# Turning the softmax rows of the first and the last attention tiles on TensorE, and storing the last block tile by tile

## The chip, the cores and the metric

The kernel runs on one core of a Trainium2 chip. The metric is the device time of one execution in microseconds. Engines are named as in the profile: PE is TensorE (PEld its weight loads), DVE is VectorE, ACT is ScalarE, POOL is GpSimd, SP is SyncE; a "q" behind a name is that engine's instruction queue, which also issues DMAs.

## The reference

The input x has 2 batches of 2048 rows and 256 columns in float32. Two layers follow one another, each on the layer norm of x:

```
x = x + attn0(xn) + moe(xn)        # layer 0: causal attention, 8 routed + 2 shared SwiGLU experts
x = x + attn1(xn) + chosen(xn)     # layer 1: causal attention, a block on the 255 best rows of each batch

def attn(x):
    q, k, v = x @ Wq, x @ Wk, x @ Wv          # layer 0 with biases, layer 1 with an output product
    s = where(causal, q @ k.T, -inf) / 16
    return softmax(s) @ v
```

## The kernel before

**Attention.** Both layers call one function, `attention` (L236). A tile is 128 query rows of one batch, 16 tiles a batch. `in_turn` (L366) takes batch 0 upwards, tiles 0 to 15, then batch 1 downwards, tiles 15 to 0, so the first and the last tiles are the shortest. The row of tile i has (i + 1) x 128 columns, cut into chunks of up to 512. `scores` (L246) multiplies queries by the normed rows on TensorE (L256), adds the causal mask to the last 128 columns, and lets VectorE scale the chunk into an SBUF buffer `row` (L267; two such buffers); ScalarE takes the exponential over the whole row (L275).

To average the values, the probabilities are needed the other way round, keys on the partitions. This is done without TensorE: `turn` (L299) has GpSimd split the float32 words of each chunk into two planes of 16-bit halves (L306), SyncE transposes both by one DMA (L308), and `join` (L280) puts the halves together as `pT`, one by VectorE (L286) and one by ScalarE (L287). `average` (L314) multiplies `pT` by the values (L321), and VectorE adds the scaled result to x (L333). Averages are held back: the oldest pending tile is averaged once at least three chunks are pending besides the newest tile's (`pending`), so the turning has other tiles' work to lie beside. After the last tile the three tiles still pending are averaged one after the other.

**Work beside it.** `piece` (L292) is called after each chunk and runs steps of generators in `side`: in layer 0, layer norm, values and gate logits of later blocks of 512 rows (`prepare0`, L483), then the routing of the experts; in layer 1, the chosen block of batch 1 and `write_back`. In layer 0 each of the first tiles also lets ScalarE issue two stores that clear scratch memory (`clear_some`, L464, and L438, 768 KB each). `project_q0` (L629) and `project_q1` (L1497) make the queries of a block once its first tile comes.

**What is shared.** PSUM has banks by tag, two for each tag (`bank`, L67): "mm" for projections, transposes and all side work, "sc" and "tr" for scores, "pv" for averages. `evacuate` (L150) copies a bank to SBUF, by VectorE and by ScalarE in turn, counted over the whole program.

**Order.** The program is traced in the order of the code, and a planner then sets the order in each engine's queue from the dependencies and its own estimates. A few dependencies are written by hand: `lead` names the main work, the joins and some DMAs are kept behind it.

**The end.** After `attention` of layer 1 a loop stores the eight blocks of x, 512 KB each, on SyncE's queue (L1521, L1522). Block 4 holds tiles 3 to 0 of batch 1 and is finished last.

Of the kernel before, what the change touches and what calls it, by code (L numbers as in the profile page):

```python
# [9 lines left out]
F32 = mybir.dt.float32  # L10
# [7 lines left out]
P = 128  # L18
B, S, D = 2, 2048, 256
NB = 8  # L20
BPB = NB // B
# [29 lines left out]
def transformer_kernel(ctx: ExitStack, tc: tile.TileContext, a: dict, out: bass.AP):  # L51
    nc = tc.nc
# [14 lines left out]
    def bank(tag):  # L67
        return psum.tile([P, 512], F32, tag=tag, name=f"ps_{tag}")

    x_blocks = []  # L70
# [8 lines left out]
    for g in range(NB):  # L79
        load_x(g, nc.sync)  # L80

    ident = const.tile([P, P], F32, tag="ident", name="ident")
# [5 lines left out]
        out=tri, in_=tri, compare_op=ALU.is_ge, fill=NEG, base=0, pattern=[[-1, P]], channel_multiplier=1  # L88
# [33 lines left out]
    def step():  # L122
        while side:
            traced = nc.cur_bb.bb.instructions
            n = len(traced)
            got = next(side[0], step)
            for i in nc.cur_bb.bb.instructions[n:]:
                behind(i)
            held[0] = got == HOLD
            if got is not step:  # L130
                return
            side.pop(0)
# [17 lines left out]
    def evacuate(dst, src):  # L150

        copies[0] += 1
        if copies[0] % 2:
            nc.vector.tensor_copy(dst, src)
        else:
            nc.scalar.copy(dst, src)
# [76 lines left out]
                nc.tensor.transpose(ps[:, j * P : (j + 1) * P], xn[:, j, c * P : (c + 1) * P], ident)  # L233
            evacuate(xnT[g][:, c, :], ps)

    def attention(pool, tiles, project_q, values, each, shifts=None, filling=()):  # L236

        def scores(b, i):  # L246
            g0 = b * BPB
            qT = queries[g0 + i // 4]
            row = pool.tile([P, S], F32, tag="row", name="row")
            mx = small.tile([P, 4], F32, tag="mx", name="mx")  # L250
            n = (i + 1) * P
            chunks = [(c, min(512, n - c)) for c in range(0, n, 512)]
            for k, (c, w) in enumerate(chunks):
                ps = bank(("sc", "tr")[k % 2])
                for dc in range(2):
                    product = nc.tensor.matmul(  # L256
                        ps[:, :w],
                        lhsT=qT[:, dc, (i % 4) * P : (i % 4 + 1) * P],
                        rhs=xnT[g0 + k][:, dc, :w],
                        start=(dc == 0),  # L260
                        stop=(dc == 1),
                    )
                lead(product)
                if c + w == n:
                    nc.vector.tensor_add(ps[:, w - P : w], ps[:, w - P : w], tri)
                by = 1.0 / 16.0 if shifts is None else shifts[g0 + i // 4][:, i % 4 : i % 4 + 1]
                lead(nc.vector.tensor_scalar(  # L267
                    row[:, c : c + w], ps[:, :w], by, None,
                    op0=ALU.mult if shifts is None else ALU.add, op1=ALU.max, accum_out=mx[:, k : k + 1],
                ))  # L270
                piece()
            nmx = small.tile([P, 1], F32, tag="nmx", name="nmx")
            nc.vector.tensor_reduce(nmx, mx[:, : len(chunks)], AX.X, ALU.max, negate=True)
            total = small.tile([P, 1], F32, tag="total", name="total")
            lead(nc.scalar.activation(row[:, :n], row[:, :n], AF.Exp, bias=nmx, accum_out=total))  # L275
            inv = small.tile([P, 1], F32, tag="inv", name="inv")
            nc.vector.reciprocal(inv, total)
            return b, i, row, inv, chunks

        def join(k, w, across, turned):  # L280

            pT = pool.tile([P, 512], F32, tag="pT", name="pT", bufs=6)
            words = pT[:, :w].bitcast(U16).rearrange("p (n k) -> p n k", k=2)
            flat = across.rearrange("p b n -> p (b n)")
            for i in (
                nc.vector.tensor_copy(words[:, :, 1], flat[:, :w]),  # L286
                nc.scalar.copy(words[:, :, 0], flat[:, w : 2 * w]),  # L287
            ):
                tc.add_manual_dep(i.ins, main[i.ins.engine].name, order, reason="not before it is there")
            turned[k] = pT  # L290

        def piece():  # L292

            pieces[0] += 1
            while joins and joins[0][0] <= pieces[0]:
                join(*joins.pop(0)[1:])
            beside()

        def turn(b, i, row, inv, chunks):  # L299

            turned = [None] * len(chunks)
            for k, (c, w) in enumerate(chunks):
                halves = row[:, c : c + w].bitcast(U16).rearrange("p (n k) -> p n k", k=2)
                planes = pool.tile([P, 1024], U16, tag="planes", name="planes", bufs=4)
                for h in range(2):
                    nc.gpsimd.tensor_copy(planes[:, h * w : (h + 1) * w], halves[:, :, 1 - h])  # L306
                across = pool.tile([P, 8, P], U16, tag="across", name="across", bufs=4)
                lead(nc.sync.dma_start_transpose(across[:, : 2 * w // P, :], planes[:, : 2 * w]))  # L308
                joins.append((pieces[0] + LAG + k, k, w, across, turned))
                if len(joins) == 4:  # L310
                    join(*joins.pop(0)[1:])
            return b, i, turned, inv, chunks

        def average(b, i, turned, inv, chunks):  # L314
            g0 = b * BPB
            pv = bank("pv")
            for k, (c, w) in enumerate(chunks):
                while turned[k] is None:
                    join(*joins.pop(0)[1:])
                for j in range(0, w, P):  # L320
                    product = nc.tensor.matmul(  # L321
                        pv[:, :D],
                        lhsT=turned[k][:, j : j + P],
                        rhs=values[g0 + k][:, j // P, :D],
                        start=(c + j == 0),
                        stop=(c + j == i * P),
                    )
                    if c + j == 0 and filled_up:
                        tc.add_manual_dep(product.ins, filled_up.ins.name, order, reason="the filling first")
                lead(product)  # L330
                piece()
            xt = x_blocks[g0 + i // 4][:, i % 4, :]
            nc.vector.scalar_tensor_tensor(xt, pv[:, :D], inv, xt, op0=ALU.mult, op1=ALU.add)  # L333

        queries = {}
        pending, joins, pieces = [], [], [0]
        filled_up = None
        def meet(tile):

            each(*tile)  # L340
            g = tile[0] * BPB + tile[1] // 4
            if g not in queries:
                queries[g] = project_q(g)

        meet(tiles[0])
        for tile, later in zip(tiles, tiles[1:] + [None]):
            pending.append(turn(*scores(*tile)))
            if later:
                meet(later)
            while sum(len(p[2]) for p in pending[:-1]) >= 3:  # L350
                average(*pending.pop(0))
        filling = iter(filling)
        for late in [*pending, None]:
            last, n = main[mybir.EngineType.PE], len(nc.cur_bb.bb.instructions)
            filled_up = next(filling, None)
            if filled_up:
                for i in nc.cur_bb.bb.instructions[n:]:
                    if i.engine == mybir.EngineType.PE:
                        tc.add_manual_dep(i, last.name, order, reason="not ahead of its turn")
                lead(filled_up)  # L360
            if late:
                average(*late)
        assert next(filling, None) is None
# [14 lines left out]
    with ExitStack() as l0:  # L378
# [336 lines left out]
        def fill_with_first():  # L715

            while side:
                step()
            w1, w2, _, _, xT = fetched[0]
            for h in range(0, 4, 2):  # L720
                for we_in, tag in ((w1, "sc"), (w2, "tr")):
                    first_up[h, tag], product = up(we_in, h, xT, TT, tag)
                    yield product
# [23 lines left out]
            for _ in work_of:  # L747
                pass
        side.append(side0())
        attention(work, in_turn, project_q0, values, before_tile, shifts, fill_with_first())  # L750
        assert next(clearing, None) is None
        while side:
            step()
# [761 lines left out]
        if (b, i) == in_turn[S // P + 1]:  # L1515
            finished.add(0)

    attention(att, in_turn, project_q1, values1, before_tile1)
    while side:
        step()  # L1520
    for g in range(NB):  # L1521
        nc.sync.dma_start(  # L1522
            out[g * 512 : (g + 1) * 512, :].rearrange("(j p) d -> p j d", p=P), x_blocks[g]
        )


_PI = 3.1415925
# [58 lines left out]
```

## Time and profile before

| | |
|---|---|
| time, median of 3 runs | 1511.12 us (1510.91 to 1512.03) |
| the profiled execution's own time | 1507.24 us |
| its span, first to last instruction | 1505.5 us |
| PE busy | 1448.6 us, 96% |
| DVE, ACT, POOL busy | 695.7, 440.0, 407.6 us |
| planes, L306 | 320 copies, 567 ns each |
| joins on ACT, L287 | 160 copies, 677 ns each |
| averages, L321 | 1088 matmuls of 256 columns, 380 ns each, pipelined |
| mean granted TensorE clock | 0.997 of full speed |

The page gives each engine's busy tenths in 40 equal slices of the span. A row of groups has line, engine, operation, output and inputs by the program's names, their shapes and count, then busy time and mean, and the idle time of the engine before them with what ended it. A float32 matmul appears as two instructions. In a timeline a row has its start, its duration, the queue, the line and the operation; "x4" marks several like instructions merged into one row.

### The profile page before, as it was taken

How to read it: one execution, taken by the hardware profiler on the slowest of the kernel's cores; microseconds unless marked ns; L12 is line 12 of the kernel's file. 1: busy time of each engine (PE TensorE's matmuls, PEld its weight loads, DVE VectorE, ACT ScalarE, POOL GpSimd, SP SyncE). 2: the span in 40 equal slices, each digit the busy share in tenths (PEclk: the TensorE clock that was granted, in tenths of full speed). 3: DMA queues.
4: the chain of work that ended last, by engine and by line, in shares of the span. 5: the costliest groups of instructions: out<-in, count | busy, mean ns of one | idle time of the engine just before them, and what ended most of it. 6: DMA issues, size and time to landing. Idle time of an engine off the chain costs nothing.

```text
span 1505.5 us, 17837 instructions
## 1 busy us (share of the span) xinstructions
PE 1448.6 (96%) x5796; PEld 1029.9 (68%) x5796; DVE 695.7 (46%) x2068; ACT 440.0 (29%) x831; POOL 407.6 (27%) x597
## 2 busy tenths in 40 slices
PE   6999999999999999999999999999999998999998
PEld 4566666658888888887665656566675765666665
DVE  6347432343222222222424447766546459666344
ACT  2443333332111111111121121115524433344233
POOL 3554776622111111111201221132013122421132
PEclk9999999999999999999999999999999999999999
DMA  5844665685878989873101011220004435621154
GB/s 157 257 115 112 174 149 129 136 162 149 234 221 221 274 234 301 226 208 102 33 21 43 28 43 35 65 97 29 0 14 115 109 70 123 146 51 24 35 119 101
DMA packets 288528, 182.99 MB, mean 122 GB/s; under 512 B 190928, under 2 KB 263376, under 8 KB 288432
## 3 DMA queue, kind: packets, MB, share of 16 engines
q1 hardware_dynamic: 252608, 133.90, 36.4%
q10 hardware_dynamic: 28192, 27.06, 5.7%
q0 software_dynamic: 7632, 20.86, 4.5%
q8 instruction: 48, 0.79, 0.2%
q14 instruction: 48, 0.39, 0.1%
HBM read 93.14 MB, written 45.14 MB: 92 GB/s over the span
## 4 chain that ended last, share of the span: by engine, by line
PE 29%; issue 10%; DVE 7%; POOL 3%; DMA 2%; ACT 2%; POOLq 0%; ACTq 0%; DVEq 0%; SPq 0%
PE ps_tr L1453 6%; PE ps_sc L1453 6%; PE ps_pv L1472 5%; POOL planes L306 3%; DMA across<-planes 2%; PE ps_mm L1324 2%; PE ps_mm L1286 1%; DVE x L1483 1%; PE ps_sc L256 1%; PE ps_mm L916 1%; PE ps_mm L1307 1%; PE ps_pv L321 1%; PE ps_mm L1390 1%; DVE row L267 1%; PE ps_tr L256 1%
## 5 line engine op out<-in xcount | busy, mean ns | idle before, releaser
L306 POOL COPY planes<-row 128x512 uint16<-128x512 uint16 (+3 forms) x320 | 167.1, 567 | 294.3 <-ACT row L275 280.7
L287 ACT COPY pT<-across 128x512 uint16<-128x512 uint16 (+3 forms) x160 | 106.1, 677 | 218.0 <-DMA across<-planes 209.0
L256 PE MATMUL ps_sc<-xnT,qT 128*128 128x512 f32 (+3 forms) x384 | 161.1, 541 | 2.3 <-ACT qT L638 2.2
L1442 POOL DMA_INDIRECT ya<-sorted_y,place x64 | 62.2, 972 | 307.6 <-DVE x L1483 224.7
L821 DVE SCALAR_TENSOR_TENSOR hid<-ps_tr,be,act 128x256 f32<-128x256 f32 (+1 forms) x144 | 60.9, 465 | 180.1 <-PE ps_tr L706 178.8
L820 ACT ACTIVATE act<-ps_sc,be 128x256 f32<-128x256 f32 (+1 forms) x144 | 58.6, 459 | 280.8 <-PE ps_sc L706 280.8
L321 PE MATMUL ps_pv<-v,pT 128*128 128x256 f32 x544 | 128.1, 381 | 5.5 <-ACT pT L287 4.5
L706 PE MATMUL ps_sc<-xT,rw 128*128 128x256 f32 (+1 forms) x576 | 129.6, 368 | 0.6 <-issue 0.6
L706 PE MATMUL ps_tr<-xT,rw 128*128 128x256 f32 (+1 forms) x576 | 129.4, 367 | 0.0
L321 PE MATMUL ps_pv<-vg,pT 128*128 128x256 f32 x544 | 124.5, 380 | 3.6 <-ACT pT L287 3.2
L698 POOL COPY xT<-xs 128x512 uint16<-128x512 uint16 (+1 forms) x72 | 49.1, 727 | 290.7 <-DMA xs<-sorted_x 265.4
L828 PE MATMUL ps_pv<-rw,hid 128*128 128x256 f32 x544 | 124.9, 382 | 0.0
L1453 PE MATMUL ps_sc<-xnT,sw 128*128 128x512 f32 x256 | 121.9, 594 | 1.8 <-PEq L856 1.8
L1453 PE MATMUL ps_tr<-xnT,sw 128*128 128x512 f32 x256 | 122.0, 593 | 0.0
L321 PEld LDWEIGHTS ps_pv<-vg,pT 128*128 128x128 f32 x544 | 101.8, 189 | 26.6 <-ACT pT L287 6.9
L321 PEld LDWEIGHTS ps_pv<-v,pT 128*128 128x128 f32 x544 | 101.3, 189 | 27.3 <-ACT pT L287 8.0
L1472 PE MATMUL ps_pv<-sw,hid 128*128 128x256 f32 x512 | 117.5, 380 | 0.0
L706 PEld LDWEIGHTS ps_sc<-xT,rw 128*128 128x128 f32 x576 | 105.3, 190 | 14.3 <-POOL xT L698 0.9
L706 PEld LDWEIGHTS ps_tr<-xT,rw 128*128 128x128 f32 x576 | 105.1, 190 | 13.2
L828 PEld LDWEIGHTS ps_pv<-rw,hid 128*128 128x128 f32 x544 | 99.2, 190 | 19.3 <-DVE hid L821 5.7
L1472 PEld LDWEIGHTS ps_pv<-sw,hid 128*128 128x128 f32 x512 | 96.6, 190 | 18.8 <-issue 6.2
L256 PEld LDWEIGHTS ps_sc<-xnT,qT 128*128 128x128 f32 x384 | 69.9, 190 | 56.2 <-issue 43.1
(332 smaller groups left out, 1932.2 us busy)
## 6 DMA issues: line engine op xcount, KB each, us to landing
rw<-in_rw SPq DMA_DIRECT2D x108, 512.0 KB, 4.5
sorted_x<-zero ACTq DMA_DIRECT2D x13, 768.0 KB, 6.3
sorted_y<-y SPq DMA_DIRECT2D x32, 256.0 KB, 4.2
be<-biases SPq DMA_DIRECT2D x36, 132.0 KB, 4.1
table<-xn SPq DMA_DIRECT2D x8, 514.0 KB, 3.4
x<-in_x SPq DMA_DIRECT2D x8, 512.0 KB, 6.9
gains<-zero ACTq DMA_DIRECT2D x8, 512.0 KB, 3.6
gain<-gains SPq DMA_DIRECT2D x16, 256.0 KB, 2.6
```

The costliest lines, as they stand in the source:

```text
L256: product = nc.tensor.matmul(ps[:, :w], lhsT=qT[:, dc, (i % 4) * P : (i % 4 + 1) * P], rhs=xnT[g0 + k][:, dc, :w], start=(dc == 0), stop=( ...
L287: nc.scalar.copy(words[:, :, 0], flat[:, w : 2 * w]),
L306: nc.gpsimd.tensor_copy(planes[:, h * w : (h + 1) * w], halves[:, :, 1 - h])
L321: product = nc.tensor.matmul(pv[:, :D], lhsT=turned[k][:, j : j + P], rhs=values[g0 + k][:, j // P, :D], start=(c + j == 0), stop=(c + j = ...
L698: nc.gpsimd.tensor_copy(words[:, :, :, 1 - k], xs[:, 2 * k : 2 * k + 2, :])
L706: product = nc.tensor.matmul(ps[:, k * n : (k + 1) * n], lhsT=we_in[:, dc, (h + k) * P : (h + k + 1) * P], rhs=xT[:, dc, :], start=(dc == ...
L820: activated = nc.scalar.activation(act, p1[:, at], AF.Silu, bias=b1[:, hc])
L821: nc.vector.scalar_tensor_tensor(hid[:, h + k, :], p2[:, at], b2[:, hc], act, op0=ALU.add, op1=ALU.mult)
L828: product = nc.tensor.matmul(po[:, r, :], lhsT=hid[:, hc, r * P : (r + 1) * P], rhs=w3[:, hc, :], start=(hc == 0), stop=(hc == 3),)
L1442: nc.gpsimd.indirect_dma_start(out=ya, out_offset=None, in_=sorted_y, in_offset=bass.IndirectOffsetOnAxis(ap=place[rank][:, t : t + 1], ax ...
L1453: product = nc.tensor.matmul(ps, lhsT=ww[:, dc, hc * P : (hc + 1) * P], rhs=xnT[g][:, dc, :], start=(dc == 0), stop=(dc == 1),)
L1472: product = nc.tensor.matmul(po[:, :D], lhsT=hid[:, hc, j * P : (j + 1) * P], rhs=w["sw3", n][:, hc, :], start=(hc == 0), stop=(hc == 3),)
```

## The change

`attention` takes a list of tiles, `direct`. In layer 0 it holds tiles 0 to 3 of batch 0, in layer 1 tiles 3 to 0 of batch 1; each of these rows is one chunk. For such a tile `turn` issues neither planes nor DMA nor joins, and puts the row on a list `straight`. Once the scores of the next tile have been issued (or, for the last tile, after the loop), `turn_straight` transposes the row in pieces of 128 columns on TensorE, into one bank of "mm", and one `evacuate` copies it to `pT`.

At the end, seven blocks are stored as before, block 4 behind them in four stores of 128 KB, tile 3 first.

```diff
         def turn(b, i, row, inv, chunks):
 
             turned = [None] * len(chunks)
+            if (b, i) in direct:
+                straight.append((row, chunks[0][1], turned))
+                return b, i, turned, inv, chunks
             for k, (c, w) in enumerate(chunks):
...
+        def turn_straight(row, w, turned):
+            ps = bank("mm")
+            for c in range(0, w, P):
+                nc.tensor.transpose(ps[:, c : c + P], row[:, c : c + P], ident)
+            turned[0] = pool.tile([P, 512], F32, tag="pT", name="pT", bufs=6)
+            evacuate(turned[0][:, :w], ps[:, :w])
...
         for tile, later in zip(tiles, tiles[1:] + [None]):
-            pending.append(turn(*scores(*tile)))
+            met = scores(*tile)
+            while straight:
+                turn_straight(*straight.pop(0))
+            pending.append(turn(*met))
             if later:
                 meet(later)
             while sum(len(p[2]) for p in pending[:-1]) >= 3:
                 average(*pending.pop(0))
+        while straight:
+            turn_straight(*straight.pop(0))
...
-        attention(work, in_turn, project_q0, values, before_tile, shifts, fill_with_first())
+        attention(work, in_turn, project_q0, values, before_tile, shifts, fill_with_first(), in_turn[:4])
...
-    attention(att, in_turn, project_q1, values1, before_tile1)
+    attention(att, in_turn, project_q1, values1, before_tile1, direct=in_turn[-4:])
     while side:
         step()
+    last = in_turn[-1][0] * BPB + in_turn[-1][1] // 4
     for g in range(NB):
-        nc.sync.dma_start(
-            out[g * 512 : (g + 1) * 512, :].rearrange("(j p) d -> p j d", p=P), x_blocks[g]
-        )
+        if g != last:
+            nc.sync.dma_start(
+                out[g * 512 : (g + 1) * 512, :].rearrange("(j p) d -> p j d", p=P), x_blocks[g]
+            )
+    to = out[last * 512 : (last + 1) * 512, :].rearrange("(j p) d -> p j d", p=P)
+    for j in reversed(range(4)):
+        nc.sync.dma_start(to[:, j, :], x_blocks[last][:, j, :])
```

More of the change, by code (lines that the diff above doesn't have):

```diff
@@ L234, in layernorm, with attention @@
             evacuate(xnT[g][:, c, :], ps)
-    def attention(pool, tiles, project_q, values, each, shifts=None, filling=()):
+    def attention(pool, tiles, project_q, values, each, shifts=None, filling=(), direct=()):
         def scores(b, i):
@@ L335, in attention @@
         queries = {}
-        pending, joins, pieces = [], [], [0]
+        pending, joins, pieces, straight = [], [], [0], []
         filled_up = None
```

## The prediction

> **What bounds the kernel.** I read the page first: its row of TensorE's busy tenths and the granted clock under it.
>
> ```profile
> PE   6999999999999999999999999999999998999998
> ...
> PEclk9999999999999999999999999999999999999999
> ```
>
> One slice is 37.6 us. TensorE is full in every slice but the first (6), one near 1270 us and the last (8); elsewhere other engines wait for it. Taking work off GpSimd or the DMA queues there buys nothing. The change touches just the two ragged ends, so I read those two in the timeline, and the stretches around the first for the clock.
>
> The last 20 us, cut to TensorE and what it waits for (start, duration, queue, line, operation; in brackets the idle time before it and who ended that):
>
> ```profile
> 1493.32 2.00 PE L321 MATMUL ps_pv<-v,pT 128*128 128x256 f32 x8 [0.34 <-ACT pT L287]
> ...
> 1495.07 1.41 POOL L306 COPY planes<-row 128x256 uint16<-128x256 uint16 x4 [2.50 <-ACT row L275]
> ...
> 1496.04 2.48 SPq L308 DMA_TRANSPOSE across<-planes  x2
> 1496.10 1.56 PE L321 MATMUL ps_pv<-v,pT 128*128 128x256 f32 x6 [0.78 <-ACT pT L287]
> ...
> 1499.07 1.72 PE L321 MATMUL ps_pv<-v,pT 128*128 128x256 f32 x6 [1.40 <-ACT pT L287]
> ...
> 1500.24 1.07 DVE L333 SCALAR_TENSOR_TENSOR x<-ps_pv,inv,x 128x256 f32<-128x256 f32 x2 [0.35 <-PE ps_pv L321]
> 1501.33 0.38 SPq L1522 DMA_DIRECT2D out_x<-x  x1
> ```
>
> The averages of tiles 3, 2, 1 and 0 each wait for a turned row: planes (GpSimd), then a transposing DMA, then the joining copies. The span ends 4.17 us after the last store is issued (1505.5 - 1501.33).
>
> The start is different. There TensorE waits for ScalarE, and ScalarE's queue stands behind its own clearing stores (L438):
>
> ```profile
> 40.97 0.75 DVE L267 TENSOR_SCALAR_CACHE_REDUCE row<-ps_sc,shift 128x512 f32<-128x512 f32 x1 [1.15 <-POOL planes L306]
> ...
> 41.94 2.00 ACTq L438 DMA_DIRECT2D sorted_x<-zero  x1
> ...
> 43.98 0.38 ACT L156 COPY vg<-ps_mm 128x265 f32<-128x265 f32 x1 [2.59 <-PE ps_mm L499]
> ...
> 44.91 1.91 PE L233 MATMUL ps_mm<-ident,xn 128*128 128x128 f32 x8 [1.26 <-ACT xn L227]
> ...
> 47.49 6.75 PE L634 MATMUL ps_mm<-xnT,wa 128*128 128x512 f32 x8 [0.67 <-DVE xnT L154]
> ```
>
> The eight matmuls of L634 take 6.75 us; the same eight take 3.60 us at 93.22. The stretches (length, busy times, clock, DMA) say why:
>
> ```profile
> 42.50:45.00 2.50, 1.24 (x5) 0.76 (x6) 0.33 (x3) 1.02 (x3) 0.00 (x0) 1.00 1.09 385
> 45.00:47.50 2.50, 1.67 (x9) 0.72 (x9) 0.75 (x2) 2.50 (x7) 1.11 (x2) 0.87 1.09 320
> 47.50:50.00 2.50, 2.50 (x3) 1.17 (x4) 0.01 (x1) 0.24 (x2) 2.50 (x4) 0.50 1.09 311
> ```
>
> The clock fell to half after the thin stretch, which cost 6.75 - 3.60 = 3.15 us. From 54 us on TensorE's idle gaps are four, 0.4 to 1.2 us each: what the start gains or loses is carried to the end.
>
> **The tail, re-timed.** Removed for each of the last four tiles: two planes copies, one transposing DMA, two joining copies (one on VectorE, one on ScalarE). Added: 4+3+2+1 = 10 turns on TensorE, four evacuations and three more stores. One turn: eight of L233 at 60.26 take 1.04 us with some 0.17 of pipeline tail, so 0.11 each, 1.1 us for ten. One evacuation from the copies at L154/L156: 0.68 (VectorE) or 0.59 (ScalarE) for 512 columns, down to an estimated 0.25 to 0.3 for 128. A score matmul of 512 columns steps by 0.43 us, an averaging one by 0.216 (32 in 6.91 us at L1472, same shape).
>
> From 1483.74, where tile 3's scores start, in the order that the trace has, with a turn behind the next tile's scores:
> - scores 3 and average of 5, as before: TensorE free at 1488.05. Scores 2 (4 x 0.32) to 1489.35.
> - turn 3: its row leaves ScalarE at 1488.1, so no wait: 0.44, to 1489.79; evacuated by 1490.7.
> - average 4 (10 x 0.216) to 1491.95; scores 1 (0.86) to 1492.81; turn 2 (0.33; row out by 1491.6) to 1493.14; scores 0 (0.43) to 1493.57.
> - average 3 (1.72) to 1495.29. Row 1: scores out at 1492.98, VectorE's mask, scale and maximum and ScalarE's exponential took 1.75 to 1.95 us for such tiles, so ready near 1494.9; row 0 near 1495.6. Turns 1 and 0 to 1495.73.
> - averages 2, 1, 0 (1.29 + 0.86 + 0.43) to 1498.31; result at 1498.48, VectorE's 0.48, store issued at 1499.0.
>
> Before it was 1501.33: **2.3 us gained**. This has average 3 standing ahead of turn 1. In the program turn 1 comes first, and the queues' order need not be the program's: one step's eight L233 turns at 32.96 and 34.00 have another tile's scores between them. If turn 1 stands first, TensorE waits from 1493.57 to 1494.9 with average 3 queued behind it: 1.3 us lost, gain 1.0. I take the first.
>
> Nothing else sits under the removed wait: the stored block 4 is last on SP either way (the earlier stores, 5 among them, are already issued by 1493.87).
>
> **The store.** The last 512 KB become four of 128 KB, three of which go while later tiles are averaged. To landing, on the same queue:
>
> ```profile
> out_x<-x SPq DMA_DIRECT2D x8, 512.0 KB, 3.2
> ...
> turned<-part SPq DMA_DIRECT2D x8, 256.0 KB, 2.1
> ```
>
> 128 KB alone has no quiet row. From above 3.2, from below 0.8 (a quarter of 3.2, if all went with size). The two rows lie 1.1 us apart for 256 KB, which would make 128 KB about 1.6. [...] Four issues of 0.4 to 0.57 us on SP fit between the averages (0.86 and 0.43 us apart), at worst 0.3 us late. Tail together: 2.3 + 1.0 = 3.3 us, ends 1.0 and 4.7.
>
> **The start.** Removed: planes of tiles 0 to 3 on GpSimd (0.52 + 0.74 + 0.96 + 1.17 = 3.4 us), four transposing DMAs, eight joins. Gains: (a) VectorE's wait at 40.97 is for tile 1's planes to free the row buffer; a turn could free it near 39.2, but TensorE's next step also waits for ScalarE until 43.94, so alone it is worth 0. (b) the DMA engines are full there (share 1.09), and the transposes' queue takes 9.5% of them from 35 to 54: up to 1.8 us of earlier clearing, of which what is ahead of 43.94 counts, some 0.5. (c) if the gap then closes, the clock's 3.15. Losses: (d) turns 0 to 2 (six, 0.66) fall where TensorE idles; cover gone, they cost that. Turn 3 comes after tile 4's scores (59.8 us), where TensorE is full: 0.44. (e) the turns take mm banks, of which there are two, and four evacuations take part in the alternation of VectorE and ScalarE. The first falls to ScalarE, as do values 2 and 3 of block 1 behind it; a copy behind the 2.0 us store holds its bank, and block 1's values and the next layer norm queue for it. One such hold is 0 to 2 us. I take (b) + 0.5, (d) - 0.44: **0**, ends +5 (b whole, c) and -4 (two holds).
>
> [...]
>
> **Sum.** On the profiled execution (1507.24 us: span 1505.5 and 1.74 around it): 1507.24 - 3.3 + 0 = 1503.9. The runs' median is 1511.12, 3.9 us above the profiled one; I take the same difference off it, 1511.12 - 3.3 = 1507.8, and round to **1507.7**.
>
> **Rivals.**
> 1. The start gains too (0.18): the DMA relief brings L634 to 46 us or earlier and the clock stays. 3.3 + 4 gives 1503.5. For it: the full DMA engines. [...]
> 2. The wait moves (0.18): turn 1 stands ahead of average 3 (1.3 lost) and the start loses about 1. 1511.1 - 1.0 - 1.0 + 1.0 gives some 1510; no difference that a measurement tells, which is taken as 0.2%, 3.0 us. That the change is hidden belongs here.
> 3. Slower (0.14): the mm banks at the start. With two or three turns' banks held behind ScalarE's clearing stores, L634 starts later, the half clock lasts one stretch longer. Each hold costs up to 2.0, the longer cold spell 3.15: about 1515. It decides once L634 of block 1 starts 6.3 us late, at 53.8 or after.
>
> The likeliest case (0.50) has its own range, 1506.0 to 1509.5; 0.36 of it lies below 1508.1. Faster: 0.36 + 0.18 = 0.54. Same: 0.14 + 0.18 = 0.32. Slower: 0.14. The range for 8 in 10 goes from 1502.5 (the start's whole gain) to 1512.5, leaving rival 3 and a little of 1 outside.
>
> **What would show it.** In the profile after: no planes, across or joins past about 1484 us; averages 3 to 0 without the waits of 0.34, 0.78 and 1.40; from tile 3's scores to the last store 15.3 us and not 17.6; from that store to the end 3.2 and not 4.17. At the start, L634 of block 1 within 1.5 us of 47.5, still at half clock. I am wrong if a turn waits for its row with an average ready behind it, if small stores land no sooner, or if L634 has moved by more than 3 us either way.

## The result, and the profile after

| | before | after | ratio (95% interval) |
|---|---|---|---|
| first comparison, medians of 8 and 8 runs | 1510.99 us | 1505.94 us | 0.9965 (0.9952 to 0.9979): 5.3 us |
| the same two again, 59 and 22 runs | 1509.76 us | 1506.75 us | 0.9977 (0.9967 to 0.9987): 3.5 us |

The change is faster, by 3.5 to 5.3 us: both intervals lie below 1. A ratio here and below is the recorded one, from which the gain in us is worked out; it is not the quotient of the two medians, which can differ from it (3.0 us in the second row). Two runs, one of the kernel before and one of the start alone, took 3084 and 3087 us, twice as long as all others, and the ratios leave them out. The profiled execution of after took 1504.37 us, with a span of 1502.7.

TensorE's row differs from before's in three slices. The first goes from 6 to 7 and the last from 8 to 9, the two ends that the change touches; the third, from 75 to 113 us, falls from 9 to 8:

```profile
span 1502.7 us, 17818 instructions
...
PE   7989999999999999999999999999999998999999
...
PEclk9999999999999999999999999999999999999999
```

**The tail.** The timeline of after, TensorE alone (start, duration, queue, line, operation):

```profile
1484.59 1.88 PE L257 MATMUL ps_sc<-xnT,qT 128*128 128x512 f32 x4
...
1490.19 0.60 PE L321 MATMUL ps_mm<-ident,row 128*128 128x128 f32 x4
1490.62 2.33 PE L332 MATMUL ps_pv<-v,pT 128*128 128x256 f32 x10
...
1493.65 0.49 PE L321 MATMUL ps_mm<-ident,row 128*128 128x128 f32 x3
...
1494.43 1.46 PE L332 MATMUL ps_pv<-v,pT 128*128 128x256 f32 x6
1495.73 0.44 PE L321 MATMUL ps_mm<-ident,row 128*128 128x128 f32 x2
1496.01 0.60 PE L332 MATMUL ps_pv<-v,pT 128*128 128x256 f32 x2
1496.45 0.27 PE L321 MATMUL ps_mm<-ident,row 128*128 128x128 f32 x1
1496.56 2.80 PE L332 MATMUL ps_pv<-v,pT 128*128 128x256 f32 x12
```

L257 makes scores (here tile 3's, the first row); L321 is now the turn and L332 the average. No average waits: the idle gaps of 0.34, 0.78 and 1.40 us of before are gone. Turn 1 (two pieces, at 1495.73) stands behind six of average 3's eight matmuls, and turn 0 behind all eight. The twelve matmuls of averages 2, 1 and 0 then run in one piece.

The four small stores of after, as the view of their source line has them (durations of the issue in ns, first and last start in us; then the time to landing):

```profile
L1545 SPq DMA_DIRECT2D out_x<-x x4: 333/339/345, 1497.2 to 1499.9; - x4
...
DMA to landing us min/median/max: 1.7/1.7/1.7
```

Tile 3's scores start at 1484.59 in this execution, so the last store is issued 15.3 us after them (17.6 before), and the span ends 2.8 us after that issue (4.17 before).

**The start.** The timeline of TensorE in after. L257 makes scores (the first ones of layer 0, from which times are counted below), L515 makes values, L332 averages, L233 turns the normed rows, L321 turns softmax rows, L650 makes block 1's queries:

```profile
33.28 0.82 PE L257 MATMUL ps_sc<-xnT,qT 128*128 128x128 f32 x4
...
42.09 1.16 PE L515 MATMUL ps_mm<-wvg,xnT 128*128 128x265 f32 x4 [0.53 <-DVE vg L154]
...
43.31 0.60 PE L332 MATMUL ps_pv<-vg,pT 128*128 128x256 f32 x2
...
44.99 1.02 PE L332 MATMUL ps_pv<-vg,pT 128*128 128x256 f32 x4
46.44 1.91 PE L233 MATMUL ps_mm<-ident,xn 128*128 128x128 f32 x8 [0.43 <-ACT xn L227]
49.02 0.55 PE L321 MATMUL ps_mm<-ident,row 128*128 128x128 f32 x3 [0.68 <-DVE xnT L154]
49.41 3.60 PE L650 MATMUL ps_mm<-xnT,wa 128*128 128x512 f32 x8
...
81.23 4.90 PE L515 MATMUL ps_mm<-wvg,xnT 128*128 128x265 f32 x12 [3.11 <-DVE xnT L154]
```

Gaps of 1.35 and 1.26 us have become 0.53 and 0.43: the averages of tiles 0 and 1, whose rows now come early, have moved into them. Block 1's queries take 3.60 us instead of 6.75. But 32 us later the values at 81.23 wait 3.11 us and take 4.90. Before they waited 1.24 us and took 3.35:

```profile
80.63 3.35 PE L499 MATMUL ps_mm<-wvg,xnT 128*128 128x265 f32 x12 [1.24 <-DVE xnT L154]
```

The stretches of after (length, busy us of PE, PEld, VectorE, ScalarE and GpSimd, granted clock, DMA share, GB/s) say where the clock fell:

```profile
42.50:45.00 2.50, 2.42 (x13) 1.73 (x12) 1.49 (x5) 0.98 (x3) 0.00 (x0) 1.00 1.03 349
45.00:47.50 2.50, 1.97 (x10) 1.04 (x9) 0.83 (x5) 1.99 (x5) 0.00 (x0) 1.00 1.03 338
47.50:50.00 2.50, 1.77 (x9) 1.06 (x10) 1.15 (x3) 1.53 (x4) 2.08 (x3) 1.00 1.03 348
80.00:82.50 2.50, 1.17 (x3) 0.75 (x4) 2.42 (x8) 2.11 (x4) 0.91 (x2) 0.87 0.31 109
82.50:85.00 2.50, 2.50 (x7) 1.86 (x7) 0.43 (x1) 0.17 (x1) 1.16 (x3) 0.50 1.12 264
```

In this pair of profiles the half clock has moved from 47 to 82 us. What the values wait for stands in VectorE's timeline of after:

```profile
79.79 0.45 DVE L287 COPY pT<-across 128x512 uint16<-128x512 uint16 x1 [4.70 <-DMA across<-planes]
...
80.49 0.68 DVE L154 COPY xnT<-ps_mm 128x512 f32<-128x512 f32 x1
```

The copy of the normed block (`xnT`, L154) is queued on VectorE behind a join (L287), which waits 4.70 us for a transposing DMA. Before, the same join waited 3.14 us:

```profile
79.22 0.46 DVE L286 COPY pT<-across 128x512 uint16<-128x512 uint16 x1 [3.14 <-DMA across<-planes]
```

Counted from the first scores (32.30 before, 33.28 after) this join could start at 46.9 us before and at 46.5 after. The DMA came hardly sooner; TensorE only reached it sooner, and waited longer.

### The profile page after: what moved, and what is told of

Read it like the earlier page. It is cut to its first block, busy times and chain, and to the rows that moved or that the text cites. A ratio compares the mean times of both kernels' runs of the same rounds, so it can differ in the third digit from the quotient of the medians.

```text
span 1502.7 us, 17818 instructions
## 1 busy us (share of the span) xinstructions
PE 1453.6 (97%) x5816; PEld 1033.6 (69%) x5816; DVE 696.2 (46%) x2064; ACT 437.5 (29%) x827; POOL 401.2 (27%) x581
## 4 chain that ended last, share of the span: by engine, by line
PE 32%; DVE 8%; issue 6%; DMA 3%; ACT 2%; POOL 2%; POOLq 0%; SPq 0%; ACTq 0%; DVEq 0%
PE ps_tr L1469 6%; PE ps_sc L1469 6%; PE ps_pv L1488 5%; DMA across<-planes 3%; PE ps_pv L332 2%; PE ps_sc L257 2%; PE ps_mm L1340 2%; POOL planes L310 2%; PE ps_mm L1302 2%; DVE x L1499 1%; PE ps_tr L257 1%; PE ps_mm L1518 1%; PE ps_mm L932 1%; PE ps_mm L1323 1%; DVE row L268 1%
## 5 line engine op out<-in xcount | busy, mean ns | idle before, releaser
L310 POOL COPY planes<-row 128x512 uint16<-128x512 uint16 (+3 forms) x304 | 161.1, 577 | 271.7 <-ACT row L276 254.7
L288 ACT COPY pT<-across 128x512 uint16<-128x512 uint16 (+3 forms) x152 | 101.8, 684 | 210.8 <-DMA across<-planes 196.4
L257 PE MATMUL ps_sc<-xnT,qT 128*128 128x512 f32 (+3 forms) x384 | 161.7, 541 | 0.6 <-DVE qT L154 0.6
L332 PE MATMUL ps_pv<-v,pT 128*128 128x256 f32 x544 | 127.6, 380 | 3.1 <-ACT pT L288 2.2
L332 PE MATMUL ps_pv<-vg,pT 128*128 128x256 f32 x544 | 125.2, 380 | 2.9 <-ACT pT L288 2.8
L332 PEld LDWEIGHTS ps_pv<-vg,pT 128*128 128x128 f32 x544 | 101.5, 189 | 26.1 <-ACT pT L288 7.0
L332 PEld LDWEIGHTS ps_pv<-v,pT 128*128 128x128 f32 x544 | 101.2, 190 | 23.7 <-issue 5.9
L722 PEld LDWEIGHTS ps_tr<-xT,rw 128*128 128x128 f32 x576 | 105.1, 190 | 13.2
L1476 ACT ACTIVATE act<-ps_sc,sb 128x512 f32<-128x512 f32 x64 | 43.9, 686 | 219.5 <-PE ps_sc L1469 207.5
```

Source lines behind the costliest of these rows:

```text
L257: product = nc.tensor.matmul(ps[:, :w], lhsT=qT[:, dc, (i % 4) * P : (i % 4 + 1) * P], rhs=xnT[g0 + k][:, dc, :w], start=(dc == 0), stop=( ...
L332: product = nc.tensor.matmul(pv[:, :D], lhsT=turned[k][:, j : j + P], rhs=values[g0 + k][:, j // P, :D], start=(c + j == 0), stop=(c + j = ...
L722: product = nc.tensor.matmul(ps[:, k * n : (k + 1) * n], lhsT=we_in[:, dc, (h + k) * P : (h + k + 1) * P], rhs=xT[:, dc, :], start=(dc == ...
```

## The experiments

Ratios are against the kernel before, run beside each group on its chip. The first four experiments share one chip, the next four kernels a second, the last four a third.

**The last tiles' turns and the small stores, without the start.**

```diff
-        attention(work, in_turn, project_q0, values, before_tile, shifts, fill_with_first(), in_turn[:4])
+        attention(work, in_turn, project_q0, values, before_tile, shifts, fill_with_first())
```

> Layer 1's four turned tiles and the split store; layer 0 as before. Theory A (the two ends add up): the tail alone gives what the profiles show from tile 3's scores to the end, 21.76 us before and 18.11 after, so 3.65 us, a ratio near 0.9976, and the first expert matmul starts as before, near 342.7 us. Theory B (the tail is all of it): about 5 us, a ratio near 0.9966. Theory C (most came from the start): 2 us or less.

Measured: 1506.00 us, ratio 0.9976 (0.9964 to 0.9988), 3.6 us. The tail alone gives what the prediction gave to the whole change. The size is not sharp: the medians (1506.00 against 1511.42) lie 5.4 us apart, at the end of the interval.

**The start alone.**

```diff
-    attention(att, in_turn, project_q1, values1, before_tile1, direct=in_turn[-4:])
+    attention(att, in_turn, project_q1, values1, before_tile1)
```

and the eight whole stores as before.

> Layer 0's four turned tiles alone; layer 1 and the stores as before. Theory A: 1.4 to 2.7 us faster (5.05 of the medians less 3.65 of the tail; the profiles put the first expert matmul 1.7 us earlier, 2.7 with the later first load taken off), a ratio near 0.9987; block 1's queries at full clock. Theory B: 0, the clock's 3.15 us given back at the next stall near 80 us. Theory D (the prediction's rival 3): slower by 1 or more.

Measured: 1509.21 us (1508.60 without the run of 3087), ratio 0.9994 (0.9976 to 1.0011). The interval holds a part of all three expectations; it was repeated below.

**The small stores alone**, added to the kernel before.

```diff
-    for g in range(NB):
-        nc.sync.dma_start(
...
+    for j in reversed(range(4)):
+        nc.sync.dma_start(to[:, j, :], x_blocks[last][:, j, :])
```

> The split store alone, no row turned on TensorE. Theory A: the last store issued 17.6 us after tile 3's scores as before, then 2.8 us to the end and not 4.17, as in the profile of the changed kernel: 1.4 us faster. The prediction's term: 1.0 us. Rival (the store is hidden or its issues cost as much): 0.

Measured: 1507.53 us, ratio 0.9975 (0.9963 to 0.9988): 3.8 us, more than expected and as much as turns and stores together. Its trace doesn't show 3.8: the stores of this kernel are

```profile
L1529 SPq DMA_DIRECT2D out_x<-x x4: 332/377/571, 1501.4 to 1504.2; - x4
...
DMA to landing us min/median/max: 1.8/1.9/2.0
```

Tile 3's scores start at 1486.58 here, so the last issue comes 17.6 us after them, as before, and the end 2.7 us later (span 1506.9). What the trace shows is 1.4 us. This, too, was repeated below.

**The turns of the last tiles alone**: the first diff, with the eight whole stores of before.

> Layer 1's four turned tiles with the block's store whole. Theory A: 2.3 us from tile 3's scores to the last store's issue (15.3 and not 17.6), 4.17 from there to the end as before: 2.3 us faster, ratio near 0.9985. Rival (a turn waits in TensorE's queue with an average behind it): 1.0 us.

Measured: 1508.81 us, ratio 0.9984 (0.9974 to 0.9994), 2.4 us. In its trace the last store is issued at 1502.3, 15.3 us after tile 3's scores (1486.99).

**The clearing stores later, without any turns on TensorE.** This is the kernel before with one edit: ScalarE issues the stores only from tile 4 on, two for each of tiles 4 to 15 of batch 0.

```diff
-                clear_some(2 if i < 8 and b == 0 else 1)
+                clear_some((2 if i > 3 else 0) if b == 0 else 1)
```

> The kernel before, with the clearing stores taken from tiles 1 to 3 and two each given to tiles 4 to 15. Theory A (ScalarE's queue standing behind the clearing stores thins the stretch before block 1's queries): queries of block 1 start 2 to 4 us earlier, at full clock, 3.60 us; and the whole gains up to 3 us less what the stores do to tiles 4 to 7. Rival (the stretch is thin because of GpSimd and the planes): queries as before, half clock.

Measured: 1510.68 us, ratio 1.0004 (0.9992 to 1.0016): no gain. TensorE's timeline of this kernel:

```profile
46.22 3.70 PE L634 MATMUL ps_mm<-xnT,wa 128*128 128x512 f32 x8 [1.14 <-DVE xnT L154]
...
130.76 1.19 PE L555 MATMUL ps_mm<-by,before 128*128 128x256 f32 x2 [3.73 <-POOL tiles L604]
```

Block 1's queries come 11.6 us after the first scores (15.2 before) and run at full clock: ScalarE's queue behind its clearing stores is what thins TensorE's work there. (The edit also takes the stores' load off the DMA engines ahead of the queries, which this run does not separate; but before, ScalarE's copy at 43.98 began as its store's issue ended, 41.94 + 2.00.) Yet no gain can be told at the first expert matmul: it comes 307.8 us after the first scores, where five profiles with the start of before have 303.3 to 310.4. One place where it goes is the wait of 3.73 us for GpSimd; before, that instruction waited 0.98 us.

**The averages of tiles 0 and 1 held** until block 1's queries are through, all else as in after. This tells whether it was they that kept the clock up.

```diff
...
+                    if c + j == 0 and (b, i) in direct and (b, i) < (0, 2):
+                        tc.add_manual_dep(product.ins, asked[1].name, order, reason="behind block 1's queries")
...
```

> The changed kernel, with the averages of layer 0's tiles 0 and 1 held behind the queries of block 1 by a dependency of order; the turns stay where they are. Theory A1 (the averages' real matmuls, drawn into the thin stretch, keep the clock): without them the stretch holds turns alone, the eight query matmuls of block 1 run at half clock again, 5.3 to 6.8 us instead of 3.60. Theory A2 (the thin stretch is short enough by itself): they stay at 3.60. The start then ends 1.3 us later at most, for the two averages' own time.

One execution: 1509.80 us (the kernel before 1509.89), from which no ratio can be formed. TensorE's timeline (L234 turns normed rows, L322 softmax rows, L653 makes the queries), then two stretches, ahead of the queries and over them:

```profile
48.05 1.91 PE L234 MATMUL ps_mm<-ident,xn 128*128 128x128 f32 x8 [1.30 <-ACT xn L228]
50.63 0.55 PE L322 MATMUL ps_mm<-ident,row 128*128 128x128 f32 x3 [0.68 <-DVE xnT L155]
51.02 3.60 PE L653 MATMUL ps_mm<-xnT,wa 128*128 128x512 f32 x8
```

```profile
46.70:51.02 4.32, 2.18 (x13) 1.19 (x13) 1.08 (x4) 3.52 (x8) 1.49 (x2) 1.00 1.03 342
51.02:54.50 3.48, 3.48 (x11) 1.57 (x10) 0.56 (x1) 0.69 (x1) 2.83 (x2) 1.00 1.02 338
```

For 4.3 us TensorE did turns and nothing else, and the clock stayed at 1.00; in this execution the averages were not needed. It is one execution, and the same start can go either way, as is shown below.

**Six and eight tiles of batch 0 turned by TensorE.** Rows of two chunks give two turns.

```diff
-                straight.append((row, chunks[0][1], turned))
+                straight.extend((row, k, c, w, turned) for k, (c, w) in enumerate(chunks))
...
-        attention(work, in_turn, project_q0, values, before_tile, shifts, fill_with_first(), in_turn[:4])
+        attention(work, in_turn, project_q0, values, before_tile, shifts, fill_with_first(), in_turn[:8])
```

(`in_turn[:6]` in the first of the two.)

> The changed kernel with layer 0's tiles 4 and 5 turned on TensorE too (two chunks each, 11 more turns, four more evacuations). Theory S (VectorE's joining copy of tile 5 waits for its transposing DMA, in its queue ahead of the layer norm's copy that TensorE waits for near 80 us, and so gives back what the start had won): the wait of 2.8 to 3.1 us near 80 us goes, 11 turns cost 1.2, the start ends 1.5 to 3 us earlier: 6.5 to 8 us faster than the kernel before, ratio 0.9947 to 0.9957. Theory T (the next stall takes over at once): as the changed kernel, 0.9965 to 0.9975.

> As above with tiles 4 to 7 (26 more turns, eight more evacuations). Theory S: the 2.8 us of turns begin to cost where TensorE is full, so no better than with tiles 4 and 5: ratio 0.995 to 0.997. Rival (each row kept off the DMA queue is worth more than its turns): better than with tiles 4 and 5, below 0.9947.

Measured: six 1505.66 us, ratio 0.9971 (0.9958 to 0.9983); eight 1504.69 us, 0.9971 (0.9959 to 0.9983). With six the wait near 81 us appears at 88.89 instead (2.50 us, and 4.34 us of values at a reduced clock): the next stall took over, as the second expectation had it. With eight no wait of 0.2 us or more is left between 51 and 127 us, and still the gain is 4.4 us, within what after had.

**Four kernels side by side**: after unaltered, eight tiles, the small stores alone, the start alone.

> The changed kernel itself, unaltered, beside the other three on one chip. Sum of terms as the traces have them (turns 2.5, small stores 1.4, start 0 to 1): 4.0 to 5.0 us below the kernel before, ratio 0.9967 to 0.9974. Theory P (the three terms are all there is): this less the start's turns alone is 3.5 to 4.0 us. Rival Q (small stores are worth 3.8 us, as their first comparison had it, whatever the trace's tail says): this is 6 to 7 us below, 0.9954 to 0.9960.

> The change with batch 0's first eight tiles turned by TensorE instead of four. Theory T (stalls taken away at the start are given back by later waits before 342 us): within 1.0 us of the changed kernel, either sign. Rival S (the start's stalls that it removes, 1.9 us idle and 1.5 us of half clock near 81 us, stay removed): 2 to 3.5 us below the changed kernel, ratio to the kernel before 0.9945 to 0.9955.

> The kernel before with the four small last stores alone. Theory P: what the trace's tail shows, 1.4 us below the kernel before, ratio 0.9985 to 0.9995. Rival Q: 3.8 us as measured once, ratio 0.9970 to 0.9980; then something outside the tail belongs to this edit.

> The change at the start alone (tiles 0 to 3 of layer 0 turned by TensorE; the last tiles and the stores as before). Theory A (the prediction's start: nothing reaches the end): ratio 0.9995 to 1.0010. Theory B (part of the 3.1 us won at block 1's queries stays, 1 to 2 us): ratio 0.9985 to 0.9993. In the trace block 1's queries take 3.6 us at full clock in both.

| | median | ratio | against before |
|---|---|---|---|
| after | 1506.75 us | 0.9977 (0.9967 to 0.9987) | -3.5 us |
| eight tiles | 1506.66 us | 0.9982 (0.9972 to 0.9992) | -2.7 us |
| small stores alone | 1508.20 us | 0.9987 (0.9974 to 0.9999) | -2.0 us |
| start alone | 1511.49 us | 1.0009 (0.9996 to 1.0021) | +1.4 us |

The stores' 3.8 us did not come again; 2.0 fits the trace. The start alone is not faster: a gain of 1 to 2 us lies outside its interval. After's 3.5 us is a little less than the 4.0 to 5.0 expected, which its interval holds; after less the start is 4.9 us, above the 3.5 to 4.0 expected, though the intervals are wide enough for both. No kernel here beats after by what can be told.

Eight tiles took no less time than four, yet their start is shorter. In both their profiles the first expert matmul comes 303.9 and 304.0 us after the first scores, against 307.7 and 307.8 in the two of after. In the last group their runs had a mean granted clock of 0.9948, after's 0.9959. Whether the edit itself lowers the clock later on and so hides its gain, or chance did, is not settled.

**Is the start's half clock a fixed thing?** The second profile of the small stores alone, taken in the last group, says no. Its start is that of before, down to the gaps. The timeline follows, then the stretches, laid 1.38 us later than those of before, as its first scores come that much later:

```profile
43.85 1.16 PE L499 MATMUL ps_mm<-wvg,xnT 128*128 128x265 f32 x4 [1.34 <-DVE vg L154]
...
46.27 1.91 PE L233 MATMUL ps_mm<-ident,xn 128*128 128x128 f32 x8 [1.26 <-ACT xn L227]
...
48.86 3.70 PE L634 MATMUL ps_mm<-xnT,wa 128*128 128x512 f32 x8 [0.67 <-DVE xnT L154]
...
78.94 3.35 PE L499 MATMUL ps_mm<-wvg,xnT 128*128 128x265 f32 x12 [1.24 <-DVE xnT L154]
```

```profile
43.88:46.38 2.50, 1.24 (x5) 0.76 (x6) 0.32 (x2) 1.04 (x3) 0.00 (x0) 1.00 1.09 387
46.38:48.88 2.50, 1.67 (x9) 0.72 (x9) 0.76 (x2) 2.50 (x7) 1.13 (x2) 1.00 1.09 323
48.88:51.38 2.50, 2.50 (x6) 1.22 (x7) 0.00 (x0) 0.72 (x2) 2.50 (x4) 1.00 1.08 311
```

These are the gaps of before, and TensorE's busy times of before, 1.24 and 1.67 us in 2.50; but the queries took 3.70 us at full clock where before they took 6.75. And after itself, in its second profile, kept its clock at 81 us. Its timeline, and then its stretches:

```profile
80.14 0.71 PE L515 MATMUL ps_mm<-wvg,xnT 128*128 128x265 f32 x2 [2.71 <-DVE xnT L154]
81.03 2.50 PE L515 MATMUL ps_mm<-wvg,xnT 128*128 128x265 f32 x10 [0.18 <-ACT xnT L156]
```

```profile
80.00:82.50 2.50, 2.18 (x9) 1.56 (x10) 1.77 (x6) 1.65 (x4) 1.92 (x4) 1.00 0.72 249
82.50:85.00 2.50, 2.50 (x11) 1.78 (x10) 0.43 (x1) 0.38 (x1) 0.14 (x1) 1.00 1.14 242
```

So the start has to be read over several profiles: five without the turns of layer 0 and five with four tiles turned. From their timelines (us; "queries" is the duration of block 1's, "wait" the one ahead of the values near 80 us):

| kernel | first scores to queries | queries | wait | clock near 82 | first scores to first expert matmul |
|---|---|---|---|---|---|
| before | 15.2 | 6.75 | 1.24 | full | 310.4 |
| turns and stores at the end | 15.9 | 6.61 | 1.23 | full | 308.9 |
| small stores alone, twice | 15.2, 15.2 | 6.57, 3.70 | 1.18, 1.24 | full | 306.3, 303.3 |
| turns at the end alone | 15.4 | 5.28 | 1.24 | full | 307.3 |
| after, twice | 16.1, 16.1 | 3.60, 3.60 | 3.11, 2.71 | half, full | 307.7, 307.8 |
| start alone, twice | 16.5, 16.4 | 3.60, 3.60 | 2.83, 2.59 | full, half | 304.9, 307.8 |
| averages 0 and 1 held | 16.2 | 3.60 | 3.08 | half | 308.9 |

## Why the prediction was right, and where it wasn't

**The sum held.** It was 3.3 us, on the tail, and 0 at the start. The two comparisons gave 5.3 and 3.5 us, the tail alone 3.6, the start alone 0.9 less and 1.4 more than before. The predicted 1507.7 lies 1.8 us above the median of 8 runs and 1.0 above that of 22; but part of this nearness is luck, as the start came to 0 by errors that cancelled.

**The tail, step by step.** From tile 3's scores to the last store's issue 15.3 us were predicted, and all eight profiles with turns at the end show 15.3, against 17.4 to 17.6 in the six without. The step that was chosen between two orders, average 3 ahead of turn 1, came as taken: six of its eight matmuls stood ahead. Pieces follow one another by 0.11 us as counted: turn 3 starts at 1490.19 and the averages behind it at 1490.62, 0.43 us for four. One turn alone lasts 0.27 us (at 1496.45), more than its share of that path.

**The store** stands in the sum with 1.0 us, 3.2 less a landing of 2.2 us for 128 KB, and no run shows that landing. In after a 128 KB store landed in 1.7 us (1.8 to 2.0 in the kernel with the stores alone). From its issue to the end were 2.7 to 3.0 us in nine profiles, against 3.9 to 4.2 in five profiles with the whole stores: 1.2 us on the mean, 1.4 in the pair before and after. The term was too small by 0.2 to 0.4; the slope between the two rows of before, 1.6 us for 128 KB, was nearer to the 1.7 than the 2.2 that was taken.

**The start: the right number by the wrong steps.** Three of its steps failed, and they cancelled.
- (c), "the clock's 3.15" us, was left out of the sum. Block 1's queries ran at full clock in all five profiles with four tiles turned, and at half for a part at least in four of five without. Over these profiles that is 5.78 - 3.60 = 2.2 us won on the mean. That the queries would stay at half clock was the author's estimate. Before, TensorE did eight turns and nothing else between 43.65 and 47.49 us, and the clock fell (0.87 from 45.00 to 47.50, then 0.50); one profile with turns alone for 4.3 us kept its clock (1.00), and so did the small stores alone on a stretch exactly as thin as that of before (1.24 and 1.67 of 2.50 us busy). "L634 still at half clock" was wrong. Its start, within 1.5 us of 47.5 expected, came 1.9 us later on the clock of the trace and 0.9 later counted from the first scores.
- (d) was 0.44 us, "turns 0 to 2 fall where TensorE idles". The queries came 0.9 us later after the first scores. In after 0.39 of it is turn 2, which stands right ahead of them (49.02 to 49.41), and the rest the layer norm, whose turns begin 13.2 us after the first scores instead of 12.6.
- "From 54 us on TensorE's idle gaps are four" holds up to 131 us only; up to the first expert matmul at 342.7 there are nine of 0.36 us or more, 9.3 us in all. So "what the start gains or loses is carried to the end" left out that later waits move with it. The wait near 80 us grew from 1.2 to 2.9 us on the mean (1.6 lost), and in three of five profiles the clock fell behind it (4.90 instead of 3.35 us, so 0.9 on the mean).

The change of these terms together is -2.2 + 0.9 + 1.6 + 0.9 = +1.2 us, a loss. Taken directly, from the first scores to the end of the values near 80 us, the means of five and five profiles are 50.9 and 51.6: 0.7 us lost, so the four terms are not quite all. At the first expert matmul the means are 307.3 and 307.4 us: nothing, in a scatter of 303.3 to 310.4.

That nothing has two parts. Summed as (1 - granted clock) x length over the stretches from the first scores to there, the clock cost 3.4 us on the mean without the turns and 1.0 with them; without this cost the way would have taken 303.8 and 306.4. By this estimate the clock's gain stayed, and the waits and turns took as much. Which of the later waits take it in each case is not settled; they change from one execution to another. The later clearing stores, which were earlier still at the queries, show no gain there either, in the one profile that they have.

**Rivals.** The first, that the start gains too, had one half of its mechanism (the clock stays) and not its result; its sum, 1511.12 - 7.3, is 1503.8 and not 1503.5. The second's wait at turn 1 didn't appear: its weight load waited 0.25 us for the row, while a matmul ran. Nor did the third's holds: block 1's queries started 1.9 us later and not 6.3, and between 34 and 100 us the clearing stores were issued in 0.53 to 1.71 us in after, 0.53 to 2.47 before.

## What to carry to other kernels

The chain of copies and DMAs that other tiles' work covers in the middle of this kernel made TensorE wait at its end, 0.34, 0.78 and 1.40 us, where no other tile covers it. There the order of the work can be re-timed from the durations in the trace: the predicted 15.3 us to the last store came out as 15.3. A gain at the start is not a gain of the kernel until the waits behind it are re-timed as well: here the queries took 3.60 us instead of 6.75, and TensorE reached the next late transfer sooner and waited 3.11 us for it instead of 1.24. And before a difference of 2 or 3 us is put down to an edit, compare the granted clock of the runs, and read a second profile of the same code.

## What was not expected of the hardware

**The half clock comes in some executions of the same code and not in others, and most of the scatter goes with it.** It comes in pieces of 3.4 us. Before the last matmul the 14 profiles have it at 36 places; summed over stretches of 2.5 us, 27 of these have 3.4 us at half clock, eight have 6.8 and one 10.25. An example: in the second profile of after the stretches from 1270 and 1272.5 us have 0.54 and 0.78: (0.46 + 0.22) x 2.5 = 1.7 us of clock lost, which is 3.4 us at half. In the profile before, the stretches from 45 to 55 have 0.87, 0.50, 0.50 and 0.77, 6.8 us at half, twice as much. Most fall at a few weak places (near 47, 82, 1270 and 1395 us), in some executions and not in others. The second profile of the start alone, with a span of 1511.2 us, has it at three of these:

```profile
82.50:85.00 2.50, 2.50 (x7) 1.87 (x7) 0.44 (x1) 0.14 (x1) 1.13 (x3) 0.50 1.11 261
...
1272.50:1275.00 2.50, 2.50 (x8) 0.77 (x7) 2.50 (x4) 0.34 (x1) 0.00 (x0) 0.50 1.15 264
...
1397.50:1400.00 2.50, 2.50 (x8) 1.96 (x7) 0.00 (x0) 0.00 (x0) 0.00 (x0) 0.50 0.02 7
```

The code at the last two is the same in all these kernels. Near 1270 us TensorE idles for 3.5 us in one piece in each of the 14, and the clock fell there in 12; near 1395 us, where gaps of 1.8 and 0.7 us stand ahead of it, it fell in six.

Over the 59 runs of the kernel before in the last group, time and mean granted clock go together with a correlation of -0.85, 1.1 us for each 0.001. By that, of the 3.8 us of the small stores 1.7 is clock: their runs had 0.0015 more than those of the kernel before beside them (0.9958 and 0.9943), and 0.0001 more when it was repeated. By the same reckoning 1.0 of after's 3.5 us in the last group is clock (0.9959 and 0.9951), and the start alone, which had 0.0015 more in its first comparison, would have been slower there too. This is a reckoning, not an experiment; and where an edit changes how often the clock falls, its share belongs to the edit.

What makes the clock fall these runs do not tell. Near 1270 us, with 3.5 us idle in one piece, it fell in 12 of the 14 profiles. At the start the gaps ahead of the half clock were at most 1.35 us before, with TensorE busy for 1.24 of 2.50 us in one stretch and 1.67 in the next; the small stores' second profile, with the same 1.24 and 1.67 of 2.50 us, went by without.
